# TensorE's order written out in the third and fourth layer of a four-layer graph network kernel

## The chip, the cores and the metric

The kernel runs on one core of a Trainium2 chip. The time is the device time of one execution, in microseconds (us), as the median of several. Five engines of the core take part: TensorE (PE, matmuls and transposes, which write PSUM), VectorE (DVE), ScalarE (ACT), GpSimd (POOL) and SyncE (SP, which issues transfers). Each has its own queue of instructions and waits for the others by semaphores. The profile shows a matmul's loading of weights apart, as PEld.

## What is computed

Four attention layers run one after the other over 4096 nodes with 256 features, all under the same 4096 x 4096 adjacency matrix, all in float32. Each adds its result to its input and normalises the rows:

```python
x = _layernorm(x + _L0_gnn_ref(x, adj, ...))   # 4 heads, additive scores
x = _layernorm(x + _L1_gnn_ref(x, adj, ...))   # 4 heads, dot-product scores
x = _layernorm(x + _L2_gnn_ref(x, adj, W, a))  # 1 head, additive scores
x = _layernorm(x + _L3_gnn_ref(x, adj, Wq, Wk))
```

The third and the fourth matter here:

```python
# third
h = x @ W
e = h @ a[:D, 0][:, None] + (h @ a[D:, 0])[None, :]
e = where(e > 0, e, 0.01 * e)
out = elu(softmax(where(adj > 0, e, -1e12)) @ h)
# fourth
Qn, Kn = cos_normalize(x @ Wq.T), cos_normalize(x @ Wk.T)
att = softmax(where(adj > 0, Kn @ Qn.T, -9e15))
out = 0.5 * (att @ x) + 0.5 * x
```

## The kernel before

The rows are held in SBUF as `X`, 32 tiles of 128 rows, in 8 blocks of 512 (`QB` = 4 tiles). A layer's main loop runs over *units*: block b of 512 target rows, tile j of 128 neighbours. A unit makes weights of 128 x 512 on ScalarE and VectorE (`weights`) and then sums them on TensorE against the neighbours' values (`sums`), into accumulators in PSUM.

**Third layer** (`additive_one`, from L382). ScalarE makes `e` (L430), VectorE multiplies it by the mask into `prob` (L432, three buffers), and TensorE does four sums of 257 columns per unit (L438), one accumulator bank for each tile of the block; the blocks use two sets of four banks in turn, `pa` and `ps`. `sums` runs one unit behind `weights`. Before a block's tiles can be neighbours it is prepared: transposed (`transposed_block`, L112 to 121: eight transposes, then one copy on VectorE and one on ScalarE) and projected (`additive_values`, L177), and the row of its source terms is filled, for blocks 0 and 1 by transposes of a broadcast (L420), for the others by a transfer. Blocks 0 and 1 are prepared ahead of the loop, and block n at tile 4(n - 2) + 2 of block 0.

Two neighbours of this layer overlap it. The second layer's last outputs (`tail` of `multi_head_attention`, L737 to 748) run at unit (0, 2): two sums of denominators on GpSimd, a sum over rows on TensorE (L654), its transposes (L661), those of the result (L668), divisions, residual and normalisation. And in the last block the preparations of the fourth layer, blocks 0 to 5, run at tiles 2, 6, ..., 22 (`Cosine.prepare`, L776 to 803): transposes; projections (L787), each PSUM tile `pr` of one bank taking two of the block's four tiles (t = 0 and 1); ScalarE's squares with a sum along the row (L791), VectorE's copy into `rows` (L793), an inverse root, a product (L798), and eight transposes of the scaled rows (L802) that ScalarE copies into `T` (L803).

**Fourth layer** (`cosine_attention`, L805 to 874). The score of a unit is a matmul of 512 columns (L826); ScalarE takes its exponential (L829), VectorE applies the mask (L830), and TensorE sums (L837), two units behind. There is one set of four accumulators. At a block's end VectorE empties them (`outputs`, L846 and L847) and normalises. Blocks 6 and 7 are prepared at units (0, 1) and (0, 12).

The order on each engine comes from the framework's planner, which simulates the program with costs of its own and takes what is ready. Where `tc.manual_schedule` names an engine, the text's order is kept on that engine. Layer 1 does so for TensorE, and the second layer's main loop for TensorE, VectorE and ScalarE. Layers 3 and 4 leave it to the planner.

Of the kernel before, what the change touches and what calls it, by code (L numbers as in the profile page):

```python
# [9 lines left out]
FP = mybir.dt.float32  # L10
# [8 lines left out]
P = 128  # L19
D = 256  # L20
# [8 lines left out]
def kernel(  # L29
# [352 lines left out]
    def additive_one(w_sb, slope, tail, op, follow):  # L382
# [3 lines left out]
        with ExitStack() as lay:  # L386
# [15 lines left out]
            def bank():  # L402
                return ps.tile([P, QW], FP, name="g")

            def turn(b):
                return transposed_block(sb, bank, b)

            def prepare(b, xT):
                groups = [(k, 1, bank().rearrange("p (n f) -> p n f", n=1)) for k in range(QB)]
                additive_values(xT, b, groups, w_sb, V, src, dst, 1, slope)  # L410
                part = row[:, b * QW:(b + 1) * QW]
                if b > 1:

                    far = dr.tile([QB, P], FP, name="far")
                    nc.gpsimd.dma_start(far.rearrange("k p -> p k"), src[:, b * QB:(b + 1) * QB, 0])
                    nc.gpsimd.dma_start(part, far.rearrange("k p -> (k p)").unsqueeze(0).to_broadcast([P, QW]))
                    return
                pr = bank()
                for k in range(QB):
                    nc.tensor.transpose(pr[:, k * P:(k + 1) * P], src[:, b * QB + k, :].to_broadcast([P, P]), ident)  # L420
                nc.scalar.copy(part, pr)
# [12 lines left out]
            def sums(b, j):  # L434
                if j == 0:
                    acc[b] = [bank() if b % 2 else pa.tile([P, QW], FP, name=f"acc{k}") for k in range(QB)]
                for k in range(QB):
                    nc.tensor.matmul(acc[b][k][:, :D + 1], prob[b, j][:, k * P:(k + 1) * P], V[:, j, :],  # L438
                                     start=(j == 0), stop=(j == NT - 1))
# [16 lines left out]
                n = next(even) % QB  # L456
                return pa.tile([P, QW], FP, name=f"acc{n}")

            for b, xT in enumerate([turn(0), turn(1)]):
                prepare(b, xT)  # L460
            even = itertools.count()
            units = [(b, j) for b in range(NB) for j in range(NT)]
            for i in range(len(units) + 1):
                if i < len(units):
                    b, j = units[i]
                    weights(b, j)
                    if b == 0 and j % QB == 2 and j // QB + 2 < NB:
                        prepare(j // QB + 2, turn(j // QB + 2))
                if i:
                    b, j = units[i - 1]  # L470
                    sums(b, j)
                    if (b, j) == (0, 2):
                        tail(bank)
                        follow.start()
                    if b and j % 4 == 0 and j // 4 < QB:
                        outputs(b - 1, j // 4)
                    if b == NB - 1 and j in (6, 10, 14):
                        follow.load_mask(0, (j - 6) // 4, prob[b, j][:, :1])

                    if b == NB - 1 and j % 4 == 2 and j // 4 < NB - 2:  # L480
                        follow.prepare(even_bank, j // 4)
                    if j == NT - 1:
                        take_all(b)

        def tail(bank):
            for k in range(QB):
                outputs(NB - 1, k)
# [3 lines left out]
    def multi_head_attention(w_sb, b_sb, tail, rows_of_den, narrow_edges):  # L491
# [12 lines left out]
        with ExitStack() as lay:  # L504
# [7 lines left out]
            with ExitStack() as pro:  # L512
# [8 lines left out]
                def bank():  # L521
                    return ps.tile([P, QW], FP, name="g")
# [108 lines left out]
            def sums(b, j):  # L631
                if j == 0:
                    acc[b] = [pa.tile([P, QW], FP, name=f"acc{c}") for c in range(KC)]
                for r in range(KC):
                    for c in range(KC):
                        half = slice(c * d, (c + 1) * d)
                        nc.tensor.matmul(acc[b][c][r * d:(r + 1) * d, :], V[half, j, r * d:(r + 1) * d],  # L637
                                         prob[b, j][half, r, :], start=(j == 0), stop=(j == NH - 1))
                if j == NH - 1:

                    kept[b] = [fin1.tile([P, QW], FP, name=f"kept{c}") for c in range(KC + 1)]
                    nc.scalar.copy(kept[b][0], acc[b][0])
                    nc.vector.tensor_copy(kept[b][1], acc[b][1])

# [1 line left out]
                eng.tensor_tensor(den[b][:, 0, :], den[b][:, 0, :], den[b][:, n, :], OP.add)  # L646

            def row_sums(bank, b):
                pd = bank()
                for r in range(KC):  # L650
                    for c in range(KC):
                        h = KC * c + r
                        half = slice(c * d, (c + 1) * d)
                        nc.tensor.matmul(pd[h * G:(h + 1) * G, :], ones[half, :G], den[b][half, 0, r * QW:(r + 1) * QW],  # L654
                                         start=True, stop=True)
                nc.scalar.copy(kept[b][KC], pd)
# [77 lines left out]
                    if b > 0:  # L734
                        finish(b - 1, j)

        def tail(bank):  # L737
            b = NB - 1
            join_sums(b, 1, nc.gpsimd)
            join_sums(b, 2, nc.gpsimd)  # L740
            row_sums(bank, b)
            reciprocals(turned_row_sums(bank, b), b)
            for k in (0, 2):
                half(turned_half(bank, b, k), b, k)
            mv = fin.tile([P, QB, 2], FP, name="mv")
            for k in range(QB):
                one_row(mv, k, X[:, b * QB + k, :D])
            layernorm_block(b, mv)
        return tail


    class Cosine:
# [2 lines left out]

        def __init__(self, stack):
            self.stack = stack

        def start(self):
            keep = self.stack.enter_context(tc.tile_pool(name="co_keep", bufs=1, side="right", reuse_waits="tile"))  # L760
# [12 lines left out]
            with behind(seen) if seen is not None else nullcontext():  # L773
                nc.gpsimd.dma_start(mask, part)  # L774

        def prepare(self, bank, b):  # L776

            in_, w_sb, T = self.pool, self.w_sb, self.T
            xT = transposed_block(in_, bank, b)
            norm = in_.tile([P, QB, 2], FP, name="norm")  # L780
            rows = in_.tile([P, QB, 2, P], FP, name="rows")
            for k in range(QB):
                t = k % 2
                if t == 0:
                    pr = bank().rearrange("p (t n f) -> p t n f", t=2, f=P)
                for c in range(KC):
                    nc.tensor.matmul(pr[:, t, :, :], xT[:, c, k * P:(k + 1) * P], w_sb[:, c, :],  # L787
                                     start=(c == 0), stop=(c == KC - 1))
                for n in range(2):
                    sq = in_.tile([P, P], FP, name="sq")  # L790
                    nc.scalar.activation(sq, pr[:, t, n, :], AF.Square, accum_out=norm[:, k, n:n + 1])  # L791
                if t:
                    nc.vector.tensor_copy(rows[:, k - 1:k + 1], pr)  # L793
            v = in_.tile([P, QB * 2], FP, name="v")
            nc.vector.tensor_scalar_max(v, norm.rearrange("p k n -> p (k n)"), 1e-8)
            r = inverse_root(v, QB * 2)
            flat = rows.rearrange("p k n f -> p (k n) f")
            nc.vector.tensor_tensor(flat, flat, r.unsqueeze(2).to_broadcast([P, QB * 2, P]), OP.mult)  # L798
            for n in range(2):
                pt = bank()  # L800
                for k in range(QB):
                    nc.tensor.transpose(pt[:, k * P:(k + 1) * P], rows[:, k, n, :], ident)  # L802
                nc.scalar.copy(T[:, n, b * QW:(b + 1) * QW], pt)  # L803

    def cosine_attention(co, tail):  # L805
        MJ = co.MJ
        T, in_ = co.T, co.pool
        with ExitStack() as lay:
# [42 lines left out]

            units = [(b, j) for b in range(NB) for j in range(NT)]
            LAG = 2
            for i in range(len(units) + LAG):
                if i < len(units):
                    b, j = units[i]
                    weights(b, j)
                    if (b, j) == (0, 1):
                        tail(bank)
                        co.prepare(bank, NB - 2)  # L860
                    elif (b, j) == (0, 12):
                        co.prepare(bank, NB - 1)
                if i >= LAG:
                    b, j = units[i - LAG]
                    if j == NT - 8:
                        y[b] = in_.tile([P, QB, D], FP, name="y")
                        nc.scalar.mul(y[b], X[:, b * QB:(b + 1) * QB, :D], 1.5)

                    if i < len(units):
                        sums(b, [j])  # L870
                    elif i > len(units):
                        sums(b, [j - 1, j])
                    if j == NT - 1:
                        outputs(b, QB if b < NB - 1 else 2)


    NJ = 16
# [17 lines left out]
    with ExitStack() as weights1, ExitStack() as den1, ExitStack() as weights3:  # L895
# [22 lines left out]
        tail = additive_heads(a0, 4, 0.2, early, narrow, ahead)  # L918
        tail = multi_head_attention(wm_sb, bm_sb, tail, rows_of_den, narrow_edges)

        def last(bank):
            tail(bank)
            den1.close()
        op = weights3.enter_context(tc.tile_pool(name="gb_o", bufs=QB))
        co = Cosine(weights3)
        tail2 = additive_one(w2_sb, 0.01, last, op, co)
# [35 lines left out]
```

## Time and profile before

| what | before |
|---|---|
| time, median of 3 | 2930.72 us (2930.72 to 2934.12) |
| span of the profiled run | 2930.1 us |
| VectorE, ScalarE, GpSimd busy | 67%, 57%, 32% |
| third layer, main loop | about 1735 to 2246 us |
| fourth layer | about 2246 us to the end |
| mean granted TensorE clock | 0.999 |

How to read it: the busy shares are over the whole span. The profile's slices show VectorE at 3 tenths and ScalarE at 2 in the fourth layer. The columns of a timeline line are start, length, engine, line, operation, output and inputs, shape and count; instructions of one kind in a row are merged into one line, and the length of such a line reaches to the end of its last record. A value in brackets is the idle time ahead of it and what ended it. Matmuls overlap in their pipeline, so the records of one row overlap too: what TensorE gets done is told by the distance between starts.

### The profile page before, as it was taken

The numbers are of one execution on the slowest core, as the hardware profiler recorded it, in microseconds if no ns is written. First come the engines' busy times: TensorE is split into PE (matmuls) and PEld (weight loads), VectorE is DVE, ScalarE is ACT, GpSimd is POOL, SyncE is SP. The second block draws the span as 40 slices with busy tenths as digits, with TensorE's granted clock in tenths as the row PEclk, the third lists the DMA queues.
The fourth block names the chain that finished last, engine by engine and source line by source line (L and its number), as shares of the span: only waits on it lengthen the run. The fifth ranks groups of instructions, "written<-read, shape, count | busy, mean of one in ns | idle before, by whom it ended". The sixth has DMA issues, their size and how long they took to land.

```text
span 2930.1 us, 50252 instructions
## 1 busy us (share of the span) xinstructions
PE 2911.7 (99%) x20205; PEld 1559.8 (53%) x20205; DVE 1956.5 (67%) x2537; ACT 1668.4 (57%) x2605; POOL 925.4 (32%) x647
## 2 busy tenths in 40 slices
PE   9999999999999999999999999999999999999998
PEld 5333333333633333333333358888887777777776
DVE  8899999997677777877877865555555333333333
ACT  7899999997356666666666654444444222222222
POOL 0010000100078888888889860000000000000000
PEclk9999999999999999999999999999999999999999
DMA  7566666664068888889889875444442333333331
GB/s 204 108 134 141 137 137 138 143 128 81 1 152 191 183 184 190 179 185 195 175 187 185 180 167 135 152 152 152 154 131 52 51 58 58 58 58 58 58 58 29
DMA packets 207147, 374.92 MB, mean 128 GB/s; under 512 B 15057, under 2 KB 90817, under 8 KB 206018
## 3 DMA queue, kind: packets, MB, share of 16 engines
q0 software_dynamic: 102304, 177.77, 38.4%
q1 hardware_dynamic: 104336, 193.69, 20.5%
q8 instruction: 158, 2.59, 0.3%
q14 instruction: 75, 0.61, 0.1%
q10 hardware_dynamic: 274, 0.26, 0.0%
HBM read 317.07 MB, written 21.04 MB: 115 GB/s over the span
## 4 chain that ended last, share of the span: by engine, by line
PE 97%; DVE 2%; ACT 1%; issue 0%; DVEq 0%; ACTq 0%
PE acc L274 23%; PE acc L837 15%; PE p L604 14%; PE acc L637 14%; PE acc L438 8%; PE g L438 8%; PE p L826 4%; PE g L826 3%; PE g L532 2%; PE g L177 1%; PE pv L546 1%; PE acc L787 1%; PE g L118 1%; PE acc L177 1%; DVE s L139 1%; DVE prob L616 1%
## 5 line engine op out<-in xcount | busy, mean ns | idle before, releaser
L616 DVE TENSOR_TENSOR prob<-p,mask 128x1024 f32<-128x1024 f32 x512 | 622.9, 1223 | 200.2 <-ACT p L606 195.4
L606 ACT ACTIVATE p<-p,shift 128x1024 f32<-128x1024 f32 x512 | 556.2, 1088 | 332.6 <-PE p L604 331.8
L274 PE MATMUL acc<-prob,V 128*32 128x512 f32 x6144 | 664.0, 592 | 1.2 <-DVE prob L264 1.2
L623 POOL TENSOR_TENSOR den<-den,prob 128x1024 f32<-128x1024 f32 x248 | 613.3, 2473 | 80.9 <-DVE prob L616 68.2
L261 ACT ACTIVATE prob<-row,dst 128x512 f32<-128x512 f32 x1020 | 633.2, 713 | 0.1
L264 DVE SCALAR_TENSOR_TENSOR prob<-prob,mask 128x2048 f32<-128x2048 f32 x256 | 582.5, 2286 | 24.2 <-ACT prob L261 20.7
L604 PE MATMUL p<-qT,kT 64*64 64x512 f32 x4096 | 532.7, 590 | 5.9 <-DVE prob L616 5.9
L637 PE MATMUL acc<-prob,V 64*64 64x512 f32 x4096 | 531.4, 589 | 0.0
L837 PE MATMUL acc<-X,prob 128*128 128x257 f32 x2048 | 486.0, 380 | 0.0
L837 PEld LDWEIGHTS acc<-X,prob 128*128 128x128 f32 x2048 | 388.4, 190 | 162.2 <-issue 114.1
L830 DVE TENSOR_TENSOR prob<-prob,mask 128x512 f32<-128x512 f32 x256 | 176.3, 691 | 419.6 <-ACT prob L829 418.4
L274 PEld LDWEIGHTS acc<-prob,V 128*32 128x32 f32 x6144 | 197.3, 110 | 453.0 <-issue 434.1
L91 POOL COPY tick<-prob 128x1 f32<-128x1 f32 x35 | 39.7, 1134 | 1020.6 <-DVE prob L264 644.0
L430 ACT ACTIVATE e<-row,dst 128x512 f32<-128x512 f32 x256 | 184.2, 721 | 234.2 <-DVE prob L432 206.7
L637 PEld LDWEIGHTS acc<-prob,V 64*64 64x64 f32 x4096 | 155.8, 133 | 285.4 <-issue 278.1
L604 PEld LDWEIGHTS p<-qT,kT 64*64 64x64 f32 x4096 | 153.7, 133 | 287.8 <-issue 260.5
L432 DVE SCALAR_TENSOR_TENSOR prob<-e,mask 128x512 f32<-128x512 f32 x256 | 176.2, 688 | 174.4 <-PE acc L438 93.5
L774 POOL DMA_DIRECT2D mask<-in_adjT x64 | 47.4, 741 | 639.5 <-DVE prob L830 509.7
L829 ACT ACTIVATE prob<-p 128x512 f32<-128x512 f32 x144 | 85.9, 596 | 257.0 <-PE p L826 243.1
L629 POOL DMA_DIRECT2D den<-prob x240 | 221.2, 922 | 24.1 <-DVE prob L616 19.7
L438 PE MATMUL g<-V,prob 128*128 128x257 f32 x1024 | 226.6, 380 | 0.0
L438 PE MATMUL acc<-V,prob 128*128 128x257 f32 x1024 | 225.3, 380 | 0.0
(154 smaller groups left out, 1975.2 us busy)
## 6 DMA issues: line engine op xcount, KB each, us to landing
mask<-in_adjT SPq DMA_DIRECT2D x256, 512.0 KB
den<-prob POOLq DMA_DIRECT2D x240, 512.0 KB, 5.2
mask<-edges SPq DMA_DIRECT2D x256, 128.0 KB
mask<-in_adjT POOLq DMA_DIRECT2D x64, 512.0 KB, 5.7
edges<-in_adj POOLq DMA_DIRECT2D x32, 512.0 KB, 9.7
den<-prob SPq DMA_DIRECT2D x16, 512.0 KB
row<-far SPq DMA_DIRECT2D x7, 1024.0 KB
X<-in_x SPq DMA_DIRECT2D x7, 512.0 KB
```

Source lines behind the costliest of these rows:

```text
L261: nc.scalar.activation(z[:, h, :], r, AF.Relu, bias=-1.0, scale=dst[:, j, h:h + 1])
L264: nc.vector.scalar_tensor_tensor(z, z, 1.0, mask[m][:, j % MJ, :].unsqueeze(1).to_broadcast([P, H, QW]), OP.add, OP.mult)
L274: nc.tensor.matmul(acc[b][h * G:(h + 1) * G, n, :], part, prob[b, j][:, h, :], start=(j == 0), stop=(j == NT - 1))
L438: nc.tensor.matmul(acc[b][k][:, :D + 1], prob[b, j][:, k * P:(k + 1) * P], V[:, j, :], start=(j == 0), stop=(j == NT - 1))
L604: nc.tensor.matmul(p[c * d:(c + 1) * d, r, :], kT[half, c, j * d:(j + 1) * d], qT[half, c, cols], start=True, stop=True)
L606: nc.scalar.activation(p, p, AF.Exp, bias=shift)
L616: nc.vector.tensor_tensor(z, p, mask[m][:, j % MJ, :].unsqueeze(1).to_broadcast([P, KC, QW]), OP.mult)
L623: nc.gpsimd.tensor_tensor(to, to, flat, OP.add)
L629: nc.gpsimd.dma_start(to, flat, accum_op=OP.add)
L637: nc.tensor.matmul(acc[b][c][r * d:(r + 1) * d, :], V[half, j, r * d:(r + 1) * d], prob[b, j][half, r, :], start=(j == 0), stop=(j == NH - 1))
L826: nc.tensor.matmul(p, T[:, 0, j * P:(j + 1) * P], T[:, 1, cols], start=True, stop=True)
L837: nc.tensor.matmul(acc[b][k], prob[b, j][:, k * P:(k + 1) * P], X[:, j, :], start=(j == 0), stop=(j == NT - 1))
```

## The change

The third and the fourth layer's loops go under `tc.manual_schedule` for TensorE. Since the planner then can't put other work between dependent parts of a preparation, the preparations are cut into steps by hand, some units apart: transposes, projections, and for the fourth layer the transposes of the scaled rows. The steps of `Cosine.prepare` come at tiles 0, 2 and 5 after a start, every fourth tile in layer 3's last block, and from tiles 1 and 12 in the fourth layer. The third layer's own preparations transpose at tile 4(n - 2) and project at 4(n - 2) + 2. Ahead of its loop, the row fill of block 0 goes between two halves of block 1's projection. The second layer's last outputs become three steps, at tiles 0, 3 and 5. What is computed, and with which instructions, stays as it was.

```diff
-            def prepare(b, xT):
-                groups = [(k, 1, bank().rearrange("p (n f) -> p n f", n=1)) for k in range(QB)]
+            def project(b, xT, ks=range(QB)):
+                groups = [(k, 1, bank().rearrange("p (n f) -> p n f", n=1)) for k in ks]
                 additive_values(xT, b, groups, w_sb, V, src, dst, 1, slope)
+
+            def fill_row(b):
...
-            for i in range(len(units) + 1):
...
-                    if b == 0 and j % QB == 2 and j // QB + 2 < NB:
-                        prepare(j // QB + 2, turn(j // QB + 2))
...
+            with tc.manual_schedule(engines={mybir.EngineType.PE}):
+                xTs = {0: turn(0), 1: turn(1)}
+                project(0, xTs[0])
+                project(1, xTs[1], [0, 1])
+                fill_row(0)
+                project(1, xTs[1], [2, 3])
+                fill_row(1)
+                for i in range(len(units) + 1):
+                    if i < len(units):
+                        b, j = units[i]
+                        weights(b, j)
+                        if b == 0 and j // QB + 2 < NB:
+                            n = j // QB + 2
+                            if j % QB == 0:
+                                xTs[n] = turn(n)
+                            elif j % QB == 2:
+                                project(n, xTs[n])
+                                fill_row(n)
+                    if i:
+                        b, j = units[i - 1]
+                        sums(b, j)
+                        if b == 0 and j in (0, 3, 5):
+                            tail(bank, (0, 3, 5).index(j))
...
+                        if b == NB - 1:
...
+                            for step, first in enumerate((0, 2, 5)):
+                                if j >= first and (j - first) % 4 == 0 and (j - first) // 4 < NB - 2:
+                                    follow.prepare(even_bank, (j - first) // 4, step)
...
-        def tail(bank):
+        def tail(bank, step):
             b = NB - 1
...
+            if step == 0:
+                join_sums(b, 1, nc.gpsimd)
+                join_sums(b, 2, nc.gpsimd)
+            elif step == 1:
+                row_sums(bank, b)
+            else:
+                pd = turned_row_sums(bank, b)
+                pos = {k: turned_half(bank, b, k) for k in (0, 2)}
+                reciprocals(pd, b)
...
-        def prepare(self, bank, b):
+        def prepare(self, bank, b, step):
...
+            if step == 0:
+                self.xT[b] = transposed_block(in_, bank, b)
+            elif step == 1:
+                xT = self.xT.pop(b)
...
+                for k in range(QB):
+                    t = k % 2
+                    if t == 0:
+                        pr = bank().rearrange("p (t n f) -> p t n f", t=2, f=P)
+                    for c in range(KC):
+                        nc.tensor.matmul(pr[:, t, :, :], xT[:, c, k * P:(k + 1) * P], w_sb[:, c, :],
+                                         start=(c == 0), stop=(c == KC - 1))
+                    for n in range(2):
+                        sq = in_.tile([P, P], FP, name="sq")
+                        nc.scalar.activation(sq, pr[:, t, n, :], AF.Square, accum_out=norm[:, k, n:n + 1])
+                    if t:
+                        nc.vector.tensor_copy(rows[:, k - 1:k + 1], pr)
...
+            else:
+                rows = self.rows.pop(b)
                 for n in range(2):
...
             LAG = 2
-            for i in range(len(units) + LAG):
...
+            steps = {(0, j + n): (NB - 2 + b, step) for b, j in enumerate((1, 12)) for step, n in enumerate((0, 2, 5))}
+            with tc.manual_schedule(engines={mybir.EngineType.PE}):
+                for i in range(len(units) + LAG):
                     if i < len(units):
                         b, j = units[i]
                         weights(b, j)
+                        if (b, j) == (0, 1):
+                            tail(bank)
+                        if (b, j) in steps:
+                            co.prepare(bank, *steps[b, j])
```

More of the change, by code (lines that the diff above doesn't have):

```diff
@@ L457, in even_bank @@
                 return pa.tile([P, QW], FP, name=f"acc{n}")
-            for b, xT in enumerate([turn(0), turn(1)]):
-                prepare(b, xT)
             even = itertools.count()
             units = [(b, j) for b in range(NB) for j in range(NT)]
-            for i in range(len(units) + 1):
-                if i < len(units):
-                    b, j = units[i]
-                    weights(b, j)
-                    if b == 0 and j % QB == 2 and j // QB + 2 < NB:
-                        prepare(j // QB + 2, turn(j // QB + 2))
[L469 to L483, printed above, removed]
@@ new lines, in additive_one @@
+            with tc.manual_schedule(engines={mybir.EngineType.PE}):
[21 more added lines that the diff above has]
+                            tail(bank, (0, 3, 5).index(j))
+                            if j == 5:
+                                follow.start()
+                        if b and j % 4 == 0 and j // 4 < QB:
+                            outputs(b - 1, j // 4)
+                        if b == NB - 1:
+                            if j in (6, 10, 14):
+                                follow.load_mask(0, (j - 6) // 4, prob[b, j][:, :1])
+                            for step, first in enumerate((0, 2, 5)):
+                                if j >= first and (j - first) % 4 == 0 and (j - first) // 4 < NB - 2:
+                                    follow.prepare(even_bank, (j - first) // 4, step)
+                        if j == NT - 1:
+                            take_all(b)
@@ L639, in sums @@
                 if j == NH - 1:
-                    kept[b] = [fin1.tile([P, QW], FP, name=f"kept{c}") for c in range(KC + 1)]
+                    kept[b] = [fin1.tile([P, QW], FP, name=f"kept{c}") for c in range(KC)]
                     nc.scalar.copy(kept[b][0], acc[b][0])
@@ L648, in row_sums @@
             def row_sums(bank, b):
+                kept[b].append(fin1.tile([P, QW], FP, name=f"kept{KC}"))
                 pd = bank()
@@ L735, in multi_head_attention @@
                         finish(b - 1, j)
-        def tail(bank):
+        def tail(bank, step):
             b = NB - 1
[L739 to L748, printed above, removed]
+            if step == 0:
[7 more added lines that the diff above has]
+                reciprocals(pd, b)
+                for k, po in pos.items():
+                    half(po, b, k)
+                mv = fin.tile([P, QB, 2], FP, name="mv")
+                for k in range(QB):
+                    one_row(mv, k, X[:, b * QB + k, :D])
+                layernorm_block(b, mv)
         return tail
@@ L757, in __init__ @@
             self.stack = stack
+            self.xT, self.rows = {}, {}
         def start(self):
@@ L774, in load_mask @@
                 nc.gpsimd.dma_start(mask, part)
-        def prepare(self, bank, b):
+        def prepare(self, bank, b, step):
             in_, w_sb, T = self.pool, self.w_sb, self.T
[L779 to L788, printed above, removed]
-                for n in range(2):
[L790 to L803, printed above, removed]
@@ new lines, in prepare @@
+            if step == 0:
+                self.xT[b] = transposed_block(in_, bank, b)
+            elif step == 1:
+                xT = self.xT.pop(b)
+                norm = in_.tile([P, QB, 2], FP, name="norm")
+                rows = self.rows[b] = in_.tile([P, QB, 2, P], FP, name="rows")
+                for k in range(QB):
+                    t = k % 2
[9 more added lines that the diff above has]
+                        nc.vector.tensor_copy(rows[:, k - 1:k + 1], pr)
+                v = in_.tile([P, QB * 2], FP, name="v")
+                nc.vector.tensor_scalar_max(v, norm.rearrange("p k n -> p (k n)"), 1e-8)
+                r = inverse_root(v, QB * 2)
+                flat = rows.rearrange("p k n f -> p (k n) f")
+                nc.vector.tensor_tensor(flat, flat, r.unsqueeze(2).to_broadcast([P, QB * 2, P]), OP.mult)
+            else:
+                rows = self.rows.pop(b)
+                for n in range(2):
+                    pt = bank()
+                    for k in range(QB):
+                        nc.tensor.transpose(pt[:, k * P:(k + 1) * P], rows[:, k, n, :], ident)
+                    nc.scalar.copy(T[:, n, b * QW:(b + 1) * QW], pt)
@@ L853, in cosine_attention @@
             LAG = 2
-            for i in range(len(units) + LAG):
[L855 to L867, printed above, removed]
-                    if i < len(units):
[L870 to L874, printed above, removed]
+            steps = {(0, j + n): (NB - 2 + b, step) for b, j in enumerate((1, 12)) for step, n in enumerate((0, 2, 5))}
+            with tc.manual_schedule(engines={mybir.EngineType.PE}):
+                for i in range(len(units) + LAG):
+                    if i < len(units):
+                        b, j = units[i]
+                        weights(b, j)
+                        if (b, j) == (0, 1):
+                            tail(bank)
+                        if (b, j) in steps:
+                            co.prepare(bank, *steps[b, j])
+                    if i >= LAG:
+                        b, j = units[i - LAG]
+                        if j == NT - 8:
+                            y[b] = in_.tile([P, QB, D], FP, name="y")
+                            nc.scalar.mul(y[b], X[:, b * QB:(b + 1) * QB, :D], 1.5)
+                        if i < len(units):
+                            sums(b, [j])
+                        elif i > len(units):
+                            sums(b, [j - 1, j])
+                        if j == NT - 1:
+                            outputs(b, QB if b < NB - 1 else 2)
     NJ = 16
@@ L919, with last @@
         tail = multi_head_attention(wm_sb, bm_sb, tail, rows_of_den, narrow_edges)
-        def last(bank):
-            tail(bank)
-            den1.close()
+        def last(bank, step):
+            tail(bank, step)
+            if step == 2:
+                den1.close()
         op = weights3.enter_context(tc.tile_pool(name="gb_o", bufs=QB))
```

## The prediction

> **What bounds the kernel now.** I read the page first: shares, slices, chain.
>
> ```profile
> PE 2911.7 (99%) x20205; PEld 1559.8 (53%) x20205; DVE 1956.5 (67%) x2537; ACT 1668.4 (57%) x2605; POOL 925.4 (32%) x647
> PE 97%; DVE 2%; ACT 1%; issue 0%; DVEq 0%; ACTq 0%
> ```
>
> TensorE is busy for 99% and is 97% of the chain, so the kernel gains only what TensorE loses. The busy share hides short losses, because a matmul's record (380 ns for 257 columns) is longer than the spacing of two in a row. The spacing comes from the chain in order of time, where a block of layer 3 is 256 records of L438 in 55.51 us: **0.217 us** each (a float32 matmul leaves two records). In the same way a 128-column transpose steps 0.109, a 256-column projection 0.216, a 512-column score 0.43. Counting records against elapsed time then shows the loss. The timeline of TensorE over one preparation in layer 3's last block:
>
> ```profile
> 2172.49 1.04 PE L118 MATMUL acc<-ident,X 128*128 128x128 f32 x8
> 2173.36 1.03 PE L438 MATMUL g<-V,prob 128*128 128x257 f32 x4
> 2174.26 3.08 PE L787 MATMUL acc<-w_sb,xT 128*128 128x256 f32 x12
> 2177.17 1.46 PE L438 MATMUL g<-V,prob 128*128 128x257 f32 x6
> 2178.63 1.13 PE L787 MATMUL acc<-w_sb,xT 128*128 128x256 f32 x4
> 2179.59 4.50 PE L438 MATMUL g<-V,prob 128*128 128x257 f32 x20
> 2184.14 1.07 PE L802 MATMUL acc<-ident,rows 128*128 128x128 f32 x8
> 2185.05 0.60 PE L438 MATMUL g<-V,prob 128*128 128x257 f32 x2
> 2185.48 0.27 PE L118 MATMUL acc<-ident,X 128*128 128x128 f32 x1
> ```
>
> The work is 16 x 0.109 + 32 x 0.217 + 16 x 0.216 = 12.14 us, and the period is 2185.48 - 2172.49 = 12.99: 0.85 lost, six times, **5.1 us**. The two preparations in layer 4 (2247.68 to 2263.06, and 2280.77 to 2292.76) lose 1.1 and 0.7 by the same count. From 1725.63 to 1800, the second layer's last outputs and six of layer 3's preparations, it is about 1.8. In between the steps are whole. So the changed stages lose 5.1 + 1.8 + 1.8 = **8.7 us**, and that is the most that the change can win.
>
> **What the Trainium skill says.** "TensorE: Matmul & The Clock Gate", Step-by-step: what each phase is for: only weight loads are pulled ahead, matmuls stay in program order. Layer 1, already in fixed order, agrees: four sums units (x96), eight transposes, x12 and x4 projections, again and again. "PSUM — Partial Sum Buffer", PSUM bank collisions raise a hardware error: two engines may not touch one bank and quadrant at once, so such accesses must be guarded. The trace shows such a guard where it matters, in the view of L787's line (us waited, times):
>
> ```profile
> its engine sat idle before it (us, times) until:
>   ACT sq L791: 5.6, 16
>   ACT xT L120: 1.7, 6
> ```
>
> Sixteen is two per preparation, eight preparations. A projection tile holds **two** 128-row parts (t = 0, 1) in one bank; ScalarE squares part 0 out of it, and the matmul of part 1 into it has to wait. ScalarE's timeline:
>
> ```profile
> 2175.53 0.28 ACT L791 ACTIVATE sq<-acc 128x128 f32<-128x128 f32 x1 [0.79 <-PE acc L787]
> 2175.70 0.19 ACT L791 ACTIVATION_READ_ACCUMULATOR sq<-acc 128x1 f32 x1
> 2175.79 0.27 ACT L791 ACTIVATE sq<-acc 128x128 f32<-128x128 f32 x1
> 2175.95 0.20 ACT L791 ACTIVATION_READ_ACCUMULATOR sq<-acc 128x1 f32 x1
> ```
>
> The last read ends at 2176.15, and TensorE's next group of L787 starts at 2176.20 by its weight load. Today the planner goes round it: the x12 are parts 0, 2 and 1 (2 goes to the other bank), and six sums stand ahead of part 3. In the text the order is 0, 1, 2, 3, and the change fixes TensorE to the text.
>
> **The change part by part.**
>
> *Transposes, projections, turned rows as steps (0, 2, 5).* Units of sums (1.73 us in layer 3, 2.59 in layer 4) stand between a step and the next. The copy of a transposed block (0.66) hides behind two units: all waits on xT go. The row chain (copy, maximum, roots, 1.2 us product) took 4.4 us from the last projection (2179.60) to the turned rows; three units are 5.2 us, so I cost it at nothing but 0.5 us in all, for blocks where the outputs of block 6 sit in VectorE's queue.
>
> *The projection step in fixed order: the loss.* Part 0 takes 4 x 0.216 = 0.86; its last record ends 0.16 later; ScalarE starts 0.04 after that (2175.49 to 2175.53), needs 0.63 for both squares, and 0.05 on TensorE is free: 1.75 after the step began instead of 0.86. Then the weight load, which could not be pulled ahead, is exposed: the skill's "LDWEIGHTS (loading the stationary operand)", columns / 1.2, gives an estimated 107 ns; the first group after such a wait is recorded at 0.48 instead of 0.38, the same 0.10. Hold: 0.88 + 0.10 = **0.98 us**, with nothing else allowed on TensorE. Part 2 has a free bank, part 3 again waits 0.98.
> In layer 3 ScalarE also makes e. In the steady state (timeline at 1902.30) a unit's end frees VectorE for prob at +0.27 and ScalarE for e at +0.99, for 0.72. The squares are ready at 1.07, so if e is first they start at 1.78, and the first hold is 1.78 + 0.63 + 0.05 - 0.86 + 0.10 = 1.70. Bounds: 0.98 and 1.70. I take e first in four of six blocks: 4 x (1.70 + 0.98) + 2 x 1.96 = 14.6. In layer 4 the exponential (0.6) is over by then: 2 x 1.96 = 3.9. Sum **18.5 us**. Queued behind the held matmul are all later sums; VectorE and ScalarE wait for those through prob's three buffers, so nothing uses the time.
>
> *Layer 4's main loop in fixed order.* Between blocks the four accumulators must be emptied by VectorE. TensorE and VectorE at such a boundary:
>
> ```profile
> 2508.74 1.02 PE L826 MATMUL p<-T 128*128 128x512 f32 x2
> 2509.60 1.03 PE L837 MATMUL acc<-X,prob 128*128 128x257 f32 x4
> 2510.47 1.02 PE L826 MATMUL g<-T 128*128 128x512 f32 x2
> 2511.32 2.77 PE L837 MATMUL acc<-X,prob 128*128 128x257 f32 x12
> ```
> ```profile
> 2510.15 0.47 DVE L847 SCALAR_TENSOR_TENSOR y<-acc,rden,y 128x256 f32<-128x256 f32 x1
> ...
> 2511.00 0.47 DVE L847 SCALAR_TENSOR_TENSOR y<-acc,rden,y 128x256 f32<-128x256 f32 x1
> ```
>
> Now the next score goes between the second and third accumulator and buys 0.86 us. In the text's order the third is due at 2510.47, freed at 2510.62 + 0.05, plus 0.10 for weights; the fourth is then due at 2511.21 and freed at 2511.52, plus 0.10: ends 0.72 later. Seven boundaries: **5.0 us**. If VectorE did not put a 0.69 us mask product ahead of the first L847, as it does today, it would be 0. I keep 5.0, since that product becomes ready at the same moment; low end 0.
>
> *Layer 3's opening and its preparations.* Projecting half of block 1 between block 0's projection and its row fill hides the first fill. The second fill follows the last projection at once and waits for one exponential: some 0.4. The tail in three steps removes the waits on joined sums and kept. I leave 0.8 of the 1.8.
>
> *No cost:* pool joins (GpSimd, two of 2.4 us, hidden by three units), kept's later allocation, longer-lived xT and rows. No transfer is added.
>
> **Sum.** After: 18.5 + 5.0 + 0.8 + 0.5 = 24.8 us lost, before 8.7: +16.1. 2930.7 + 16.1 = **2946.8 us**.
>
> **Rivals.**
> 1. *Milder*: ScalarE is free for every square and VectorE frees the accumulators in time. 16 x 0.98 = 15.7, + 0.8 + 0.5 - 8.7 = +8.3: 2939.0. For it: the order on ScalarE and VectorE is still planned, and e beats the squares by only 0.08 us. With one of the two true, 2942 to 2944.
> 2. *Faster*: the holds don't come, because the steps leave all waits behind them; 8.7 less some 1 us left: 2923. For it: xT and row waits do vanish. Against it: the wait is inside one step, and no distance between steps reaches it.
> 3. *Worse*: with TensorE held, VectorE's row chain slips too, and the turned rows are held about 0.7 in each of eight blocks: +5.6 on top, 2952.4. For it: the slack is only 0.8 us; against it: the longer projection gives VectorE time as well.
> 4. *No change*: the holds are half as long as I make them, 16 x 0.5 + 1 - 8.7.
>
> **Chances.** Forecast (2943 to 2950) 0.50; milder 0.24; faster 0.08; worse 0.14; no change 0.04. Milder is slower by over 0.2% too (5.9 us, above 2936.6), so slower 0.87, same 0.05, faster 0.08. Range 2938 to 2952: it takes in the milder case and half of the worse one.
>
> **What would show it.** In the changed trace: the wait of the projection line on squares still 16 times, but some 18 us by the spacing of records, with TensorE in the order 4, 4, 4, 4 and gaps after the first and third; no waits on xT; blocks of layer 4 longer by 0.7 at each boundary; whole steps everywhere else. I'd be wrong if another matmul stands between parts 0 and 1, or if the square's wait is gone. Of the sizes, e ahead of the squares and the boundaries are the least sure.

## The result, and the profile after

| | before | after |
|---|---|---|
| median | 2931.51 us (2930.72 to 2934.12, 6 runs) | 2948.97 us (2948.15 to 2950.88, 6 runs) |
| ratio | | 1.0059, 95% interval 1.0046 to 1.0071 |
| span of the profiled run | 2930.1 us | 2946.6 us |

The changed kernel is slower by 17.5 us; the two profiled runs differ by 16.5. The page after, busy shares and chain:

```profile
PE 2911.1 (99%) x20205; PEld 1561.3 (53%) x20205; DVE 1959.0 (66%) x2537; ACT 1668.5 (57%) x2605; POOL 925.8 (31%) x647
PE 95%; DVE 3%; ACT 1%; issue 0%; DVEq 0%; ACTq 0%
```

As many instructions on every engine, and TensorE is as busy as before. The chain shows what is new: it now leaves TensorE for VectorE and ScalarE in 4% of the span, not 3%. Who holds it is in the view of the projection's line (L815 now, squares L819):

```profile
its engine sat idle before it (us, times) until:
  ACT sq L819: 37.4, 32
  issue: 1.0, 4
```

This view counts matmuls and weight loads, so 32 is 16 holds seen on both. These are all its lines: the waits on the transposed block are gone. The timeline of TensorE over one preparation in layer 3's last block:

```profile
2167.43 1.04 PE L118 MATMUL acc<-ident,X 128*128 128x128 f32 x8
2168.31 1.90 PE L440 MATMUL g<-V,prob 128*128 128x257 f32 x8
2170.04 1.04 PE L832 MATMUL acc<-ident,rows 128*128 128x128 f32 x8
2170.91 1.90 PE L440 MATMUL g<-V,prob 128*128 128x257 f32 x8
2172.65 1.03 PE L815 MATMUL acc<-w_sb,xT 128*128 128x256 f32 x4
2174.96 1.99 PE L815 MATMUL acc<-w_sb,xT 128*128 128x256 f32 x8 [1.28 <-ACT sq L819]
2177.73 1.13 PE L815 MATMUL acc<-w_sb,xT 128*128 128x256 f32 x4 [0.78 <-ACT sq L819]
2178.70 3.63 PE L440 MATMUL g<-V,prob 128*128 128x257 f32 x16
2182.17 0.38 PE L118 MATMUL acc<-ident,X 128*128 128x128 f32 x2
```

The work is what it was, 12.14 us, and the period is now 2182.17 - 2167.43 = 14.74: 2.60 lost instead of 0.85. The projection, once x12 and x4 with sums in between, is x4, x8, x4 with nothing in between: part 0, a hold, parts 1 and 2, a hold, part 3. Every other step is whole. ScalarE in the first hold:

```profile
2173.68 0.72 ACT L432 ACTIVATE e<-row,dst 128x512 f32<-128x512 f32 x1 [1.26 <-DVE prob L434]
2174.30 0.26 ACT L819 ACTIVATE sq<-acc 128x128 f32<-128x128 f32 x1
2174.46 0.19 ACT L819 ACTIVATION_READ_ACCUMULATOR sq<-acc 128x1 f32 x1
2174.55 0.27 ACT L819 ACTIVATE sq<-acc 128x128 f32<-128x128 f32 x1
2174.71 0.20 ACT L819 ACTIVATION_READ_ACCUMULATOR sq<-acc 128x1 f32 x1
```

e stands ahead of the squares; the last read ends at 2174.91, and TensorE goes on at 2174.96. So two things make up this hold: the bank, and in five of the six blocks an e ahead in ScalarE's queue. At a boundary of layer 4, TensorE and then VectorE's line that frees the fourth accumulator:

```profile
2521.40 1.02 PE L856 MATMUL p<-T 128*128 128x512 f32 x2
2522.26 1.84 PE L867 MATMUL acc<-X,prob 128*128 128x257 f32 x6
2524.27 0.67 PE L867 MATMUL acc<-X,prob 128*128 128x257 f32 x2 [0.17 <-DVE mv L126]
2524.78 1.02 PE L856 MATMUL g<-T 128*128 128x512 f32 x2
```
```profile
2523.66 0.46 DVE L877 SCALAR_TENSOR_TENSOR y<-acc,rden,y 128x256 f32<-128x256 f32 x1
2524.05 0.17 DVE L126 BATCH_NORM_AGGREGATE mv<-bn 128x2 f32<-128x6 f32 x1
```

Eight records of sums take 8 x 0.217 = 1.74 us, and from 2522.26 to 2524.78 are 2.52: about 0.78 lost. The idle bracket shows only 0.17 of it, since the records' modelled ends cover the rest, and it names L126, which is not the reader of the bank: L877 is, done at 2524.12.

To have one measure for all runs, I added up in each trace the distances between the starts of TensorE's records in the changed stages, less the step of each kind. It gives us lost:

| stage | before | after |
|---|---|---|
| layer 3's opening and its preparations | 1.7 | 0.9 |
| layer 3's last block (six projections) | 5.4 | 14.9 |
| layer 4's two preparations | 1.8 | 4.8 |
| layer 4's seven boundaries | under 0.3 | 5.2 |
| sum | 9.0 | 25.8 |

The difference is 16.8, where the spans differ by 16.5.

### The profile page after: what moved, and what is told of

It is laid out like the page before. It is cut to its first block, busy times and chain, and to the rows that moved or that the text cites. A ratio compares the mean times of both kernels' runs of the same rounds, so it can differ in the third digit from the quotient of the medians.

```text
span 2946.6 us, 50240 instructions
## 1 busy us (share of the span) xinstructions
PE 2911.1 (99%) x20205; PEld 1561.3 (53%) x20205; DVE 1959.0 (66%) x2537; ACT 1668.5 (57%) x2605; POOL 925.8 (31%) x647
## 4 chain that ended last, share of the span: by engine, by line
PE 95%; DVE 3%; ACT 1%; issue 0%; DVEq 0%; ACTq 0%
PE acc L274 22%; PE p L621 14%; PE acc L867 14%; PE acc L654 14%; PE acc L440 8%; PE g L440 7%; PE p L856 4%; PE g L856 3%; PE g L549 2%; PE g L177 1%; PE pv L563 1%; PE g L118 1%; PE acc L177 1%; PE acc L815 1%; DVE prob L633 1%; DVE s L139 1%
## 5 line engine op out<-in xcount | busy, mean ns | idle before, releaser
L859 ACT ACTIVATE prob<-p 128x512 f32<-128x512 f32 x144 | 85.8, 596 | 262.0 <-PE p L856 248.0
```

## The experiments

Each was timed beside the kernel before on the same chip, and the ratio is to that. Its medians were 2932.25 us (beside experiments 1 to 4), 2932.66 (6 to 9) and 2933.88 (5). The changed kernel itself was not timed again beside them, so differences from it go across sets of runs. "Lost" is the sum by spacing, as in the table.

**1. The squares after both parts.** If the hold comes from the bank that two parts share, it goes when nothing is read between them.

```diff
-                    for n in range(2):
-                        sq = in_.tile([P, P], FP, name="sq")
-                        nc.scalar.activation(sq, pr[:, t, n, :], AF.Square, accum_out=norm[:, k, n:n + 1])
                     if t:
+                        for s in range(2):
+                            for n in range(2):
+                                sq = in_.tile([P, P], FP, name="sq")
+                                nc.scalar.activation(sq, pr[:, s, n, :], AF.Square,
+                                                     accum_out=norm[:, k - 1 + s, n:n + 1])
                         nc.vector.tensor_copy(rows[:, k - 1:k + 1], pr)
```

> The changed kernel, but ScalarE's squares of both parts of a projection tile come after the matmuls of both parts, so that no matmul waits for a square in its own bank. Theory (a matmul in text order waits for the squares read from the same bank): the 16 holds of the changed kernel, 14.9 us in layer 3 and 4.8 in layer 4 by the spacing of its records, go to under 0.5 us in all: 2949.0 - 19.7 = 2929.3 us. Rival (TensorE loses because ScalarE is behind with e and exponentials, whichever bank it reads): the squares come later still, the row chain of the last step slips, and 15 to 20 us stay lost: 2945 to 2949. Second rival (cutting into steps itself costs): no change, 2949.

Measured: 2929.8 us (12 runs), ratio 0.9990, interval 0.9982 to 0.9999. Against the changed kernel 19.2 us are back by the medians, about 20 by the ratios. TensorE's timeline:

```profile
2172.68 3.62 PE L815 MATMUL acc<-w_sb,xT 128*128 128x256 f32 x16
2176.13 3.63 PE L440 MATMUL g<-V,prob 128*128 128x257 f32 x16
```

The projection is one line of sixteen with no hold. Lost in the eight preparations: nothing (0.0); at the boundaries 5.2, as before this edit. Both rivals fall: the squares came later, and neither the backlog nor the steps kept the loss.

**2. Parts in the order 0, 2, 1, 3.** This keeps the squares where they are and puts only the other bank's part in between.

```diff
-                for k in range(QB):
+                prs = {}
+                for k in (0, 2, 1, 3):
                     t = k % 2
                     if t == 0:
-                        pr = bank().rearrange("p (t n f) -> p t n f", t=2, f=P)
+                        prs[k] = bank().rearrange("p (t n f) -> p t n f", t=2, f=P)
+                    pr = prs[k - t]
```

> The changed kernel with the projection's parts in the order 0, 2, 1, 3, the planner's order before, and no other work between them. Theory: part 2 takes 0.86 us in its own bank while part 0 is squared. In layer 3, where e stands ahead of the squares, part 1 is due 1.73 us after the step began and free at about 2.3: hold 0.6 + 0.1; part 3 none. In layer 4 about 0.1. Together 6 x 0.7 + 2 x 0.1 = 4.4 us instead of 19.7: 2949.0 - 15.3 = 2933.7 us. Rival (ScalarE's backlog or the steps as such): within 3 us of 2949.

Measured: 2934.5 us, ratio 1.0007 (0.9998 to 1.0016). Lost: 3.8 in layer 3's last block, and 1.0 in layer 4's preparations where 0.2 was expected. The order of four matmul groups alone is worth 14.5 us.

```profile
2171.25 1.89 PE L817 MATMUL acc<-w_sb,xT 128*128 128x256 f32 x8
2173.56 1.99 PE L817 MATMUL acc<-w_sb,xT 128*128 128x256 f32 x8 [0.42 <-ACT sq L821]
```

Two parts run, then one short hold: due at 2171.25 + 1.73 = 2172.98, started 0.58 later. Part 2 doesn't wait, since it has a tile of its own. In this kernel such a tile is a whole bank, so no run tells whether the wait goes by the bank or by the tile.

**3. Every square twice.** The dose: the same holds, longer squares.

```diff
                         sq = in_.tile([P, P], FP, name="sq")
                         nc.scalar.activation(sq, pr[:, t, n, :], AF.Square, accum_out=norm[:, k, n:n + 1])
+                        sq = in_.tile([P, P], FP, name="sq")
+                        nc.scalar.activation(sq, pr[:, t, n, :], AF.Square, accum_out=spare[:, k, n:n + 1])
```

> The changed kernel with every square computed twice, the second time into a sum that nobody uses. ScalarE gets 64 more activations with their reads, 0.31 us each by the changed kernel's timeline, 20 us in all, where it is idle for 43% of the time. Theory: each of the 16 holds grows by the 0.63 us of two squares, 16 x 0.63 = +10.1: 2959.1 us. Rival (holds come from e or exponentials in ScalarE's queue, or from the steps): under +2 us, since ScalarE has room.

Measured: 2960.2 us (4 runs), ratio 1.0093 (1.0076 to 1.0110): 11.2 above the changed kernel by the medians, about 10.0 by the ratios. Lost in the preparations: 22.2 and 7.3, 9.8 more than the changed kernel's 14.9 and 4.8; sixteen times two squares with their reads at 0.63 are 10.1. In the projection of the same block as above:

```profile
2175.17 1.03 PE L816 MATMUL acc<-w_sb,xT 128*128 128x256 f32 x4
2177.99 1.99 PE L816 MATMUL acc<-w_sb,xT 128*128 128x256 f32 x8 [1.80 <-ACT sq L822]
2181.45 1.13 PE L816 MATMUL acc<-w_sb,xT 128*128 128x256 f32 x4 [1.46 <-ACT sq L822]
```

From x4 to x8 are 2.82 us, not 2.31, and from x8 to x4 3.46, not 2.77. Of the 20 us of added squares half come back in the time: those of parts 0 and 2, because a matmul stands behind them. Those of parts 1 and 3 cost next to nothing. So on an engine that is busy for 57% some squares have their full price and others almost none.

**4. The steps with the planner's order.** The same edit twice, in layer 3 and in layer 4.

```diff
-            with tc.manual_schedule(engines={mybir.EngineType.PE}):
+            with nullcontext():
```

> The changed kernel with its steps, but without the fixed order of TensorE in layers 3 and 4: the planner orders TensorE again. Theory: the steps were never the loss. The planner puts other work between the parts, the waits on the transposed block and on the scaled rows are gone with the distance, and the boundaries of layer 4 are filled again: the loss in these stages falls from 25.9 us to 2 to 5, below the 9.0 of the kernel before: 2925 to 2929 us. Rival (the cutting into steps costs): 2945 to 2949.

Measured: 2930.0 us, ratio 0.9992 (0.9985 to 0.9998). The steps don't cost, so the rival falls; but the time is above the 2925 to 2929 that I gave, with about 6.9 us lost in all where I gave 2 to 5. Lost in layer 3's last block: 5.5, as much as before. Why is seen in the timeline:

```profile
2172.07 1.89 PE L815 MATMUL acc<-w_sb,xT 128*128 128x256 f32 x8
2173.80 0.60 PE L440 MATMUL g<-V,prob 128*128 128x257 f32 x2
2174.38 1.13 PE L815 MATMUL acc<-w_sb,xT 128*128 128x256 f32 x4
2175.35 1.46 PE L440 MATMUL g<-V,prob 128*128 128x257 f32 x6
2176.81 1.13 PE L815 MATMUL acc<-w_sb,xT 128*128 128x256 f32 x4
2177.77 1.90 PE L440 MATMUL g<-V,prob 128*128 128x257 f32 x8
2179.51 1.04 PE L118 MATMUL acc<-ident,X 128*128 128x128 f32 x8
2180.38 2.33 PE L440 MATMUL g<-V,prob 128*128 128x257 f32 x10
2182.96 0.30 PE L832 MATMUL acc<-ident,rows 128*128 128x128 f32 x1 [0.25 <-DVE rows L826]
```
```profile
2181.59 1.22 DVE L826 TENSOR_TENSOR rows<-rows,r 128x1024 f32<-128x1024 f32 x1
```

The planner fills the parts' waits with 2 + 6 records of sums, and six of these are then missing between the projection and the turned rows: 18 stand there, where the text has 24. The product that scales the rows (VectorE, L826) ends at 2182.81, 5.04 after the projection (2177.77), and 18 records with eight transposes take 4.78. So 2.4 of the 5.5 us are waits on the scaled rows. Nearly all of the other 3.1 are waits on the squares, which 2 and 6 records don't quite cover: 0.15 and 0.16 here, with 0.10 after each.

**5. The planner with steps and late squares.** I ran this last, to see whether fixing the order earns anything once the holds are out. It is experiments 1 and 4 together.

> The changed kernel's steps with the planner's order of TensorE and with late squares: against late squares and score between, 2923.7 us, it lacks only the fixed order. Theory (fixing the order is worth something once no hold is in it, because the planner puts the turned rows' transposes some 0.4 us ahead of their product): the waits on squares go, those on rows stay at about 2.4 to 3.3 us in layer 3's last block, with 0.8 in the opening and 0.4 in layer 4: 4.3 us lost of the kernel before's 9.0, 2927.9 us. Rival (the late squares were the whole gain, and the order doesn't matter): 2923 to 2925.

Measured: 2924.3 us, ratio 0.9969 (0.9958 to 0.9979). My theory fell and the rival was right: the waits on rows went too. With no part to wait for, the planner leaves the steps as the text has them:

```profile
2171.10 3.62 PE L815 MATMUL acc<-w_sb,xT 128*128 128x256 f32 x16
2174.55 3.63 PE L440 MATMUL g<-V,prob 128*128 128x257 f32 x16
2178.02 1.04 PE L118 MATMUL acc<-ident,X 128*128 128x128 f32 x8
2178.89 1.90 PE L440 MATMUL g<-V,prob 128*128 128x257 f32 x8
2180.63 1.04 PE L834 MATMUL acc<-ident,rows 128*128 128x128 f32 x8
```
```profile
2178.08 1.23 DVE L828 TENSOR_TENSOR rows<-rows,r 128x1024 f32<-128x1024 f32 x1
```

All 24 records stand ahead of the rows; with the transposes they take 6.08 us. The product ends 4.76 after the projection (2174.55 to 2179.31), and the 5.04 of experiment 4 would have been in time as well. So the waits on rows there came from the sums that filled the squares' waits. Why the planner chose each order is not shown.

**6. The score between the accumulators**, in the changed kernel. The helper `scores` (the score's matmul, taken out of `weights`) and the choice of accumulators in `sums` are left out here.

```diff
+                        if b and j == 0:
+                            sums(b, [j], (0, 1))
+                            scores(b, 3)
+                            sums(b, [j], (2, 3))
-                        if i < len(units):
+                        elif i < len(units):
                             sums(b, [j])
```

> The changed kernel, but at each of layer 4's seven block boundaries the score matmul of the unit after next stands between the second and the third accumulator's sums, as the planner had it before. Theory (the third and fourth sums of a new block wait for VectorE to empty their banks; 5.2 us in all by the spacing of the changed kernel's records, 0.75 per boundary): the 0.86 us of the score fill the hold, and 2949.0 - 5.2 = 2943.8 us. Rival (VectorE empties the banks later still, or the score moved ahead is missed behind): the hold stays, 2947 to 2949.

Measured: 2943.6 us, ratio 1.0037 (1.0023 to 1.0050). The boundaries' loss is gone from the trace, and the preparations' 14.9 and 4.8 stand. At the boundary:

```profile
2522.91 1.03 PE L872 MATMUL acc<-X,prob 128*128 128x257 f32 x4
2523.78 1.02 PE L853 MATMUL g<-T 128*128 128x512 f32 x2
2524.64 1.90 PE L872 MATMUL acc<-X,prob 128*128 128x257 f32 x8
```

**7. Layer 4 alone back to the planner**: the second of experiment 4's two edits.

> The changed kernel with TensorE's order fixed in layer 3 alone; layer 4's loop goes back to the planner, steps kept. Theory: the 5.2 us at layer 4's boundaries vanish, and the 4.8 us of its two preparations fall to about 0.7, what the run with all steps planned showed; layer 3 keeps its 14.9: 2949.0 - 9.3 = 2939.7 us. Rival (one cause in layer 3 delays all that follows, and layer 4 only inherits it): within 2 us of 2949.

Measured: 2939.5 us, ratio 1.0023 (1.0015 to 1.0032). Lost: 14.9 in layer 3's last block, 0.7 in layer 4's preparations, nothing at the boundaries. Layer 4 inherits nothing.

**8. Late squares and the score between**, edits 1 and 6 together.

> The changed kernel with both: ScalarE's squares after the matmuls of both parts of a tile, and the score between the second and third accumulator at layer 4's boundaries. Theory (the two losses are separate and in sequence on TensorE, so their removals add): 2949.0 - 19.7 - 5.2 = 2924.1 us, with about 1 us lost in the changed stages where the kernel before loses 9.0: 8 us under the kernel before. Rival (some of the time was on another engine's path, which now ends last): 2928 to 2930, no better than late squares alone.

Measured: 2923.7 us (6 runs), ratio 0.9969 (0.9957 to 0.9982): the two losses add, and this version beats both kernels, the kernel before beside it by 9.0 us. Lost in the changed stages: 0.9, all in the opening. Beside it the profiled run has one wait of 1.0 in the middle of layer 3, at 1822 us, that no other run shows.

**9. Late squares in the kernel before**, no steps and no fixed order; the edit is that of experiment 1.

> The kernel before, planner's order throughout and no steps, with the squares after the matmuls of both parts. The kernel before pays in each of eight preparations about 0.12 at part 1 and 0.26 at part 3 for the squares, 3.0 us in all. Theory (the squares' guard costs where nothing can be put in its place): 2932.2 - 3.0 = 2929.2 us. Rival (the planner fills with the same few sums, so the wait only moves to the transposed block or to the scaled rows): 2931 to 2933, no change.

Measured: 2931.0 us, ratio 0.9993 (0.9987 to 1.0000), at the rival's edge, and the interval holds the theory too: unclear. By spacing 6.1 us are lost instead of 9.0, the 3.0 that I gave, and the profiled span is 2.4 shorter, but the median only 1.6. Of the 3.6 left in the last block, 1.8 are waits on the scaled rows, 0.5 more than in the kernel before: part of the gain moves there, as the rival had it.

## Why the prediction was right

It gave 2946.8 us, and 2949.0 was measured; +16.1 was forecast, +17.5 came. By its steps, with the losses of the trace after:

- **What bounds the kernel**: right. Counting TensorE's records against time gives 16.8 us more lost, and the spans differ by 16.5.
- **What the change can win**: 8.7 given, 9.0 lost before by the sum over all records; 0.9 of it is left in the opening, where 0.8 was given, with the second row fill's wait for one exponential as the largest piece (0.37).
- **The holds in the projection**: right in cause (experiments 1, 2 and 3) and in number, sixteen. Layer 3: 14.6 given, 14.9 measured. That the sizes agree so well is in part luck, for two were off and cancelled. e was ahead in five of the six blocks, not four, but costs less than I gave: the first hold is 2174.96 - 2172.65 - 0.86 + 0.10 = 1.55, not 1.70. The squares start 0.62 after e's start, while its record lasts 0.72, so 1.65 after the step began. The prediction has 1.78, and its own figures, 0.99 + 0.72, give only 1.71.
- **Layer 4's preparations**: the mis-sized term, 3.9 given, 4.8 measured. I had ScalarE free there. Block 7 came as given, 0.98 for the first hold. In block 6 the first hold is 2262.53 - 2260.10 - 0.86 + 0.10 = 1.67:

```profile
2260.50 0.58 ACT L859 ACTIVATE prob<-p 128x512 f32<-128x512 f32 x1
2261.17 0.28 ACT L819 ACTIVATE sq<-g 128x128 f32<-128x128 f32 x1
2261.34 0.19 ACT L819 ACTIVATION_READ_ACCUMULATOR sq<-g 128x1 f32 x1
2261.81 0.42 ACT L192 ACTIVATE neg<-neg 128x256 f32<-128x256 f32 x1 [0.28 <-DVE neg L191]
2262.13 0.26 ACT L819 ACTIVATE sq<-g 128x128 f32<-128x128 f32 x1
2262.29 0.19 ACT L819 ACTIVATION_READ_ACCUMULATOR sq<-g 128x1 f32 x1
```

  The unit's exponential (L859) is over in time, as given: the first square starts 1.07 after the step did. What I left out is an exponential of the third layer's last outputs (L192). It stands between the two squares, and ScalarE even sits idle for 0.28 until VectorE has its input. The second square starts 0.96 after the first, where it is 0.25 in the timeline of layer 3 above.
- **Second holds**: 0.98 given, about 1.04 measured in seven of the eight blocks: 2177.73 comes 0.94 after part 3 was due, and 0.10 follows. That this 0.10 is the exposed weight load is not shown: no run tests it, and the trace records such a load at 0.19.
- **Layer 4's boundaries**: right; 0.72 each given; measured 0.78 at the boundary above, and 0.75 each by the sum over the stage, 5.2 in all. VectorE did keep the mask product ahead of the first L877 (2520.50 to 2521.19). Experiment 6 shows that the order does it: with the score back in its place the loss is gone.
- **The row chain**: 0.5 given, nothing measured; three units are enough in every block.

Of the rivals, the milder one needed ScalarE free and the accumulators emptied in time; neither was so. The faster one named what came true elsewhere: the waits on the transposed block and on the rows are gone, but no distance between steps reaches a wait inside one. The worse one did not come: the rows are never late. Nor were the holds half as long as given: none is under 0.98.

## What to carry to other kernels

When an engine's order is fixed by hand, list the pairs of instructions that the planner had put something between, and look at each for a dependency inside the step, not only between steps: here two matmul groups that share a PSUM bank, with a reader in between, cost 19 to 20 us over sixteen holds, and moving the reader behind both gave them back. Then measure the steps with the planner's order as well: steps and late squares alone gave a ratio of 0.9969, as good as the fixed order with both losses mended by hand (0.9969 too). So fixing the order itself earned nothing here. An engine that looks half idle still counts in full where a saturated one waits for it.

## What the runs showed that I had not expected

- Mending one wait removed another: with the squares late, the planner's waits on scaled rows (2.4 us, experiment 4) vanished too (experiment 5), because the sums that filled the one were the cover of the other (18 records against 24).
- The brackets of a timeline understate a hold on TensorE: 0.17 us where the spacing shows 0.78 at a boundary, and 1.28 where it is 1.45 and 0.10 for the weights.
